# One group of norms ahead of the first table, and the routing check moved among the experts of layer 2

## The chip, the core and the metric

The kernel runs on one core of a Trainium2 chip. The metric is the device time in microseconds (us) from the start to the end of one execution. The engines of the core are named as the profile names them: PE (TensorE, matmuls; PEld are its weight loads), DVE (VectorE), ACT (ScalarE), POOL (GpSimd) and SP (SyncE, which here only issues DMAs; the profile calls its queue SPq). Each engine has its own instruction stream, and the streams are tied together by semaphores.

## What is computed

The reference is a network of four layers on a graph of 3125 nodes with 256 features and 50000 edges. Each layer adds a graph convolution and a mixer to `x`, and then a feed-forward block:

```python
xn = _layernorm(x)
x = x + gnn(xn, src, dst, ...) + mix(xn)
x = x + ffn(_layernorm(x))          # layers 0 to 2; layer 3's ffn routes by its own graph
```

Three pieces matter here. Layer 0's graph convolution multiplies the normed nodes with four relation matrices (256 x 256 each), and edges then fetch rows of the result. Layer 2's feed-forward block runs six experts on all nodes, each made of three 256 x 256 products with a relu after the first two, and adds the experts' outputs with routing weights that are zero for all but the best two. Layer 3's feed-forward block has a second edge list of 32768 edges (`edge_index` of `L3_ffn`), over which it runs a small graph attention.

## The kernel before, in words

Nodes are laid out in 25 tiles of 128, and most loops go over `GROUPS`: six groups of four tiles and a last one of a single tile. The whole of `x`, its layer norm `xn` and the transposed `xnT` stay in on-chip memory. All matmuls are fp32 and most are recorded under line 110, in the helper `mm`. The trace shows each of these as two records, so x8 in a row of it are four matmuls of the program.

**The start.** `build` (L2620) loads `x` and the four relation matrices (`relw`), loads the edge lists, and then runs `norm_x`, which for each group calls `norm_tiles` (L165 to L178): statistics and scaling on DVE, a square root on ACT, eight PE transposes, and two copies of the transposed tiles by ACT and DVE. After all seven groups come the tables: `fill` (L1001) makes for each tile two products of 512 columns (each two matmuls), has ACT copy them to `htab_s`, and SP writes 512 KB to `h_tab` in DRAM. Between the third and the fourth group stands `regular` (L2370), which checks that the edges are sorted and evenly spread: DVE builds one-hot rows (`ct_oh`, L610) that PE sums (L612), PE transposes the destinations (L2335), and they go through DRAM and back (L2337, L2339) so that each can be compared with its neighbour. Its verdict `ok` decides by `tc.If` between `fast` and `general`. With these inputs `fast` runs.

**Order.** The instructions are issued as written only on POOL (`manual_schedule`). On the other engines a planner of the compiler puts them in an order of its own, from the order in which the program emits them and the dependencies. What stands in an engine's stream then is fixed.

**Layer 2's experts and the routing of layer 3.** `l2_ffn` (L1673) computes the routing weights and then loops over six experts and, in each, over seven blocks of 512 nodes (the last has 128): four matmuls of 512 columns with `w1`, four with `w2`, and for each of four tiles two of 256 columns with `w3`. ACT applies the relus (L1710), and DVE adds to `x` (L1717). In the first expert two more PE instructions per tile add a bias. In the last expert `after2` norms each block and fills two more tables, `tab3` and `self3` (L901), from which layer 3 gathers.

Beside this the 256 columns of layer 3's second edge list are scattered into sorted order: `send4` yields one indirect DMA after the other (`by_dst`, L357, 128 rows of 8 bytes each, issued by POOL). The class `Pump` (L2691) counts the columns of the products that `mm` emits, and each time the count passes its limit it takes the next scatter from the generator and makes it wait for that product:

```python
    def after(self, product, n):
        self.seen += n
        if self.seen >= self.columns:
            self.seen -= self.columns
            i = next(self.gen, None)
            if i is not None:
                ...
                self.tc.add_manual_dep(i, product.name, info, reason="in time with the products")
```

The router's products count 6400 columns, each expert's 38400.

After the experts comes `route_check` (L2086), in a pool `chk4` of its own. SP loads the sorted list back (`rec`, L696), with a wait for all 256 scatters. DVE copies the destinations to `rc_d` (L2095); PE transposes them in four pieces (L2335), each copied by ACT or DVE to `od_dc` and written to DRAM (L2337); SP loads them shifted (`od_dh`, L2339); three DVE instructions compare neighbours (`od_jk`, L2342 to L2345); PE sums the bad ones (L2361); and DVE writes `ok4` (L2364), which is read only after layer 3's gathers, at the next `tc.If`.

**Layer 3's beginning.** `seg_near` (L434) gathers rows of `tab3` on POOL (L447) and sums them on PE with one-hot matrices (L430) that DVE makes (L416). Beside it `l3_mix` takes statistics of `xn` (`l3a_st`, L149), scales (`hb`, L1791 and L1794, on DVE), and has PE transpose the result (L165) and multiply it with `wx`.

Of the kernel before, what the change touches and what calls it, by code (L numbers as in the profile page):

```python
# [33 lines left out]
GROUPS = [(t, min(4, T - t)) for t in range(0, T, 4)]  # L34
# [55 lines left out]
def wtile(ap):  # L90

    return ap.rearrange("(k p) f -> p k f", p=P)


class Net:
    def __init__(self, tc, a, out):
        self.tc, self.nc, self.a, self.out = tc, tc.nc, a, out
        self.flip = 0
        self.apart = {}
        self.one_hots = 8  # L100
        self.pump = None
# [1375 lines left out]
    def l1_ffn(self, pool, after=None):  # L1477
# [66 lines left out]
        for b0, w in BLOCKS:  # L1544
            t0, n = b0 // P, w // P
            zb = pool.tile([P, 4, D], F32, name="z", bufs=2)
            z, full = zb[:, :n], [P, n, D]
            nc.vector.tensor_add(z, self.xn[:, t0:t0 + n], b2c[:, None, :].to_broadcast(full))
            for s in range(2):
                hT = pool.tile([P, 4, 512], F32, name="hT", bufs=2)  # L1550
                for f in range(4):
                    p = self.ps(w)
                    self.mm(p, [(W1[s][:, k, f * P:(f + 1) * P], self.xnT[:, k, b0:b0 + w]) for k in range(2)])
                    nc.scalar.activation(hT[:, f, :w], p, AF.Gelu, bias=B1[s][:, f:f + 1])  # L1554
                for i in range(n):
                    p = self.ps(D)
                    self.mm(p, [(hT[:, f, i * P:(i + 1) * P], W2[s][:, f, :]) for f in range(4)])
                    behind.append((z[:, i, :], p, wts[s]))
                    if len(behind) > 1:
                        add(*behind.pop(0))  # L1560
                    yield
            add(*behind.pop(0))
            self.ln_rows(pool, lambda i: z[:, i, :], lambda i: z[:, i, :], "l1z", n)
            nc.vector.tensor_mul(z, z, gam[:, None, :].to_broadcast(full))
            nc.vector.tensor_add(z, z, bet[:, None, :].to_broadcast(full))
            nc.vector.tensor_add(self.x[:, t0:t0 + n], self.x[:, t0:t0 + n], z)
            if after is not None:
                after(t0, n)
# [104 lines left out]
    def l2_ffn(self, pool, after=None):  # L1673
# [23 lines left out]
        for e in range(NE):  # L1697
# [4 lines left out]
            for b0, n in BLOCKS:  # L1702
                h = None
                for j, b in enumerate((b1, b2)):
                    o = pool.tile([P, 2, 512], F32, name=f"h{j}", bufs=2)
                    for f in range(2):
                        p = self.ps(n)
                        self.mm(p, [(w[j][:, k, f * P:(f + 1) * P],
                                     self.xnT[:, k, b0:b0 + n] if h is None else h[:, k, :n]) for k in range(2)])
                        nc.scalar.activation(o[:, f, :n], p, AF.Relu, bias=b[:, 2 * e + f:2 * e + f + 1])  # L1710
                        yield
                    h = o
                for i in range(n // P):
                    t = b0 // P + i
                    p = self.ps(D)
                    self.mm(p, [(h[:, k, i * P:(i + 1) * P], w[2][:, k, :]) for k in range(2)])
                    nc.vector.scalar_tensor_tensor(self.x[:, t, :], p, r[:, t, e:e + 1], self.x[:, t, :],  # L1717
                                                   op0=OP.mult, op1=OP.add)
                    if e == 0:
                        p = self.ps(P, parts=NE)  # L1720
                        nc.tensor.transpose(p, r[:, t, :], self.ident)
                        rT = pool.tile([NE, P], F32, name="rT", bufs=2)
                        nc.vector.tensor_copy(rT, p)
                        p = self.ps(D)
                        nc.tensor.matmul(p, rT, b3, start=True, stop=True)
                        nc.vector.tensor_add(self.x[:, t, :], self.x[:, t, :], p)
                    yield
                if e == NE - 1 and after is not None:
                    after(b0 // P, n // P)
# [665 lines left out]
    def fast(self):  # L2395

        nc, tc, a = self.nc, self.tc, self.a
        g = self.g
        with tc.tile_pool(name="keepf", bufs=1) as keep, tc.tile_pool(name="dramf", bufs=1, space=DRAM) as dram:
            self.dram = dram  # L2400
            tp = lambda name: tc.tile_pool(name=name, bufs=1)
# [6 lines left out]
            ok4 = keep.tile([P, 1], I32, name="ok4")  # L2408
# [50 lines left out]
            with Banks(self, **plain):  # L2459
                route = tp("route")  # L2460
                rec4, place4 = self.route_lists(route.__enter__())
                by_dst = dram.tile([P * C2, 2], F32, name="by_dst")
# [3 lines left out]
                send4 = self.send(by_dst, place4, rec4, C2)  # L2466
# [33 lines left out]
            with Banks(self, **plain):  # L2500
                with tp("set3") as sp, tp("ffn2") as p:
                    tab, fill3 = self.linear_table("tab3", sp, self.load(sp, "wl", wtile(a["L3_gnn_W_lT"])))
                    own, fill_own = self.linear_table("self3", sp, self.load(sp, "wr", wtile(a["L3_gnn_W_rT"])),
                                                      self.rowb(sp, "L3_gnn_b_l"))

                    def after2(t0, n):
                        self.norm_tiles(t0, n)
                        fill3(t0, n)
                        fill_own(t0, n)
                    self.pump = Pump(tc, send4, 760)  # L2510
                    for _ in self.l2_ffn(p, after2):
                        pass
                    self.pump = None
                    for _ in send4:
                        pass
                with tp("chk4") as p:
                    self.route_check(p, by_dst, ok4)
            route.__exit__(None, None, None)
            order.__exit__(None, None, None)

# [99 lines left out]
    def build(self):  # L2620
        nc, tc, a = self.nc, self.tc, self.a
        with tc.tile_pool(name="keep", bufs=1) as keep, tc.tile_pool(name="dramk", bufs=1, space=DRAM) as dramk:
            self.keep, self.dramk = keep, dramk
            self.constants(keep)
            self.x = keep.tile([P, T, D], F32, name="x")
            for t0, n in GROUPS:
                nc.sync.dma_start(self.x[:, t0:t0 + n, :],
                                  a["x"][t0 * P:(t0 + n) * P, :].rearrange("(t p) f -> p t f", p=P))
            self.g = {"n": C1, "tiles": T, "src": self.load(keep, "e1src", a["src"], dtype=I32)}
            self.xn = keep.tile([P, T, D], F32, name="xn")  # L2630
            self.xnT = keep.tile([P, 2, NP], F32, name="xnT")
            self.ln = (keep.tile([P, T, 6], F32, name="ln_st"), keep.tile([P, T, 2], F32, name="ln_mv"),
                       keep.tile([P, T], F32, name="ln_rs"))
            self.mixed = set()
            self.rdeg = keep.tile([P, T], F32, name="rdeg")
            self.deg = keep.tile([P, T], F32, name="deg")
            with Banks(self, mm=6), tc.tile_pool(name="reg", bufs=1) as p:
                fill = self.l0_table(p)
                self.destinations(p)
                self.norm_x()  # L2640
                for i, (t0, n) in enumerate(GROUPS):
                    if i == 3:
                        ok = self.regular(p, self.g)
                    fill(t0, n)
                ok = self.value(ok)
            with tc.If(ok > 0) as branch:
                with tc.manual_schedule(engines={mybir.EngineType.Pool}):
                    self.fast()
            with branch.Else():
                self.general()  # L2650
            o = self.out[:(T - 1) * P, :].rearrange("(t p) f -> p t f", p=P)
            nc.sync.dma_start(o, self.x[:, :T - 1, :])
            nc.sync.dma_start(self.out[(T - 1) * P:, :], self.x[:TAIL, T - 1, :])
# [37 lines left out]
class Pump:  # L2691


    def __init__(self, tc, gen, columns):
        self.tc, self.gen, self.columns, self.seen = tc, gen, columns, 0

    def after(self, product, n):
        self.seen += n
        if self.seen >= self.columns:
            self.seen -= self.columns  # L2700
            i = next(self.gen, None)
            if i is not None:
                info = mybir.DependencyInfo(mybir.DependencyClass.Sync, mybir.DependencyReason.DATA)
                self.tc.add_manual_dep(i, product.name, info, reason="in time with the products")

# [91 lines left out]
```

## Time and profile before

| what | us |
|---|---|
| three runs | 4594.84, 4579.54, 4588.5 (median 4588.5) |
| the profiled execution | 4591.9 |
| its span, first to last instruction | 4590.2 |
| PE busy in it | 3616.8 (79%) |
| POOL busy in it | 2612.1 (57%) |
| DVE busy in it | 2211.5 (48%) |

By stage, from the trace (us from the start of the span):

| stage | from | to | PE busy | DVE busy | POOL busy |
|---|---|---|---|---|---|
| norms, first table, edge check | 0 | 139.7 | 113.2 | 47.4 | 5.0 |
| layers 0 and 1, gathers of layer 2 | 139.7 | 2673.5 | 1866.0 | 1444.4 | 1705.2 |
| layer 2: router and first expert | 2673.5 | 2832.8 | 139.3 | 34.7 | 57.4 |
| layer 2: experts 1 to 4 | 2832.8 | 3103.4 | 269.4 | 47.1 | 194.4 |
| layer 2: last expert, with norms and tables | 3103.4 | 3255.2 | 131.1 | 55.0 | 0.0 |
| routing check, begin of layer 3's mixer | 3255.2 | 3302.5 | 18.7 | 43.8 | 21.3 |
| layer 3: gathers and mixer | 3302.5 | 3932.0 | 547.0 | 290.2 | 364.1 |
| layer 3: feed-forward block | 3932.0 | 4590.2 | 532.3 | 249.0 | 264.6 |

A row of the timeline gives the start, the length, the engine, the line and operation, out and in tiles, the count of merged instructions, and in square brackets the idle time before it with what ended it. A busy PE is not a PE at its peak, since the ends of its matmuls are modelled.

### The profile page before, as it was taken

How to read it: one execution, taken by the hardware profiler on the slowest of the kernel's cores; microseconds unless marked ns; L12 is line 12 of the kernel's file. 1: busy time of each engine (PE TensorE's matmuls, PEld its weight loads, DVE VectorE, ACT ScalarE, POOL GpSimd, SP SyncE). 2: the span in 40 equal slices, each digit the busy share in tenths (PEclk: the TensorE clock that was granted, in tenths of full speed). 3: DMA queues.
4: the chain of work that ended last, by engine and by line, in shares of the span. 5: the costliest groups of instructions: out<-in, count | busy, mean ns of one | idle time of the engine just before them, and what ended most of it. 6: DMA issues, size and time to landing. Idle time of an engine off the chain costs nothing. (4 is left out here: it accounts for less than half of the span.)

```text
span 4590.2 us, 47080 instructions
## 1 busy us (share of the span) xinstructions
PE 3616.8 (79%) x13977; PEld 2403.7 (52%) x13977; DVE 2211.5 (48%) x7451; ACT 749.8 (16%) x1455; POOL 2612.1 (57%) x2605
## 2 busy tenths in 40 slices
PE   7889876954877867677777679998699995389898
PEld 3457543633545545455455334555476773257665
DVE  4477431145777775883545342113665233515443
ACT  2010001211100112113111011222122220013222
POOL 0577776755777747565777524770376565226550
PEclk9889977976978878788998868999799998588888
DMA  3433343314433420123333300001233233200000
GB/s 123 160 96 101 103 122 99 110 49 127 133 101 104 109 63 21 31 50 97 103 110 107 111 21 8 15 8 37 84 111 109 82 98 114 59 4 10 8 8 29
DMA packets 231200, 348.62 MB, mean 76 GB/s; under 512 B 74128, under 2 KB 168135, under 8 KB 230936
## 3 DMA queue, kind: packets, MB, share of 16 engines
q0 software_dynamic: 108384, 219.50, 17.5%
q1 hardware_dynamic: 118136, 121.97, 8.6%
q10 hardware_dynamic: 4416, 4.01, 0.3%
q8 instruction: 118, 1.93, 0.2%
q14 instruction: 146, 1.20, 0.1%
HBM read 294.62 MB, written 50.61 MB: 75 GB/s over the span
## 5 line engine op out<-in xcount | busy, mean ns | idle before, releaser
L430 PE MATMUL seg<-G,E 128*128 128x256 f32 (+1 forms) x3210 | 917.6, 417 | 217.0 <-DMA G<-tab,e3src 85.2
L430 PEld LDWEIGHTS seg<-G,E 128*128 128x128 f32 x3210 | 601.7, 202 | 500.9 <-issue 134.3
L110 PE MATMUL mm<-xnT,w 128*128 128x512 f32 (+1 forms) x1232 | 540.5, 586 | 20.9 <-DVE x L2226 20.5
L447 POOL DMA_INDIRECT G<-h_tab,gi x391 | 386.0, 987 | 264.7 <-DMA selfw<-in_L_gnn_self_W 136.9
L416 DVE TENSOR_SCALAR E<-iota_row,e1dl 128x128 f32<-128x128 f32 (+1 forms) x1173 | 365.1, 321 | 354.1 <-PE seg L430 343.5
L357 POOL DMA_INDIRECT by_src<-rec,place x391 | 419.3, 1073 | 188.9 <-PE mm L110 121.0
L447 POOL DMA_INDIRECT G<-tab,e1src x391 | 383.9, 982 | 202.6 <-PE seg L430 131.0
L842 POOL DMA_INDIRECT ring<-l1rows,e1src x391 | 423.6, 1083 | 132.0 <-issue 54.2
L447 POOL DMA_INDIRECT G<-tab,e3src x391 | 387.6, 991 | 123.3 <-PE seg L430 65.5
L430 PE MATMUL seg<-ring,E 128*128 128x264 f32 (+1 forms) x1762 | 424.5, 381 | 31.2 <-DVE E L416 21.2
L110 PE MATMUL mm<-w,hT 128*128 128x256 f32 (+1 forms) x1712 | 398.2, 385 | 0.5 <-ACT hT L1554 0.5
L357 POOL DMA_INDIRECT by_dst<-rec,place x256 | 251.5, 982 | 240.1 <-PE mm L110 196.0
L842 POOL DMA_INDIRECT ring<-l3rows,e2src x256 | 248.2, 970 | 225.8 <-PE seg L430 155.8
L430 PEld LDWEIGHTS seg<-ring,E 128*128 128x128 f32 x1762 | 309.5, 213 | 117.1 <-DVE E L416 47.5
L110 PEld LDWEIGHTS mm<-xnT,w 128*128 128x128 f32 x1232 | 236.9, 205 | 248.6 <-issue 217.8
L110 PEld LDWEIGHTS mm<-w,hT 128*128 128x128 f32 (+1 forms) x1712 | 319.0, 190 | 59.1 <-issue 16.9
L165 PE MATMUL mm<-ident,xn 128*128 128x128 f32 x400 | 95.1, 393 | 226.5 <-DVE xn L178 223.3
L418 DVE TENSOR_SCALAR E<-iota_row,e3dl,rec 128x128 f32<-128x128 f32 (+1 forms) x391 | 144.1, 381 | 218.9 <-PE seg L430 217.2
L1717 DVE SCALAR_TENSOR_TENSOR x<-mm,l2t_r,x 128x256 f32<-128x256 f32 x150 | 70.8, 482 | 299.7 <-PE mm L110 299.7
L165 PEld LDWEIGHTS mm<-ident,xn 128*128 128x128 f32 x400 | 65.9, 191 | 256.1 <-DVE xn L178 175.2
L854 DVE TENSOR_TENSOR ring<-ring,ex 128x260 f32<-128x260 f32 (+1 forms) x647 | 192.2, 319 | 2.4 <-ACT ex L834 2.3
L1710 ACT ACTIVATE h<-mm,b 128x512 f32<-128x512 f32 (+1 forms) x168 | 107.2, 641 | 361.2 <-PE mm L110 360.9
(710 smaller groups left out, 4962.5 us busy)
## 6 DMA issues: line engine op xcount, KB each, us to landing
w<-in_L_ffn_w SPq DMA_DIRECT2D x16, 1024.0 KB
h_tab<-htab_s SPq DMA_DIRECT2D x25, 512.0 KB
r_b<-rowa SPq DMA_DIRECT2D x64, 128.0 KB
bn_h<-c_h SPq DMA_DIRECT2D x50, 128.0 KB
G<-h_tab,gi POOLq DMA_INDIRECT x391
by_src<-rec,place POOLq DMA_INDIRECT x391
ring<-l1rows,e1src POOLq DMA_INDIRECT x391
G<-tab,e3src POOLq DMA_INDIRECT x391
```

The costliest lines, as they stand in the source:

```text
L110: m = self.nc.tensor.matmul(out, l, r, start=(i == 0), stop=(i == last))
L165: self.nc.tensor.transpose(p[:, i * P:(i + 1) * P], src(t0 + i)[:, k * P:(k + 1) * P], self.ident)
L357: return self.nc.gpsimd.indirect_dma_start(out=table, out_offset=bass.IndirectOffsetOnAxis(ap=idx, axis=0), in_=src, in_offset=None, bound ...
L416: self.nc.vector.tensor_scalar(e[:, :w], self.iota2[:, :w], g["dl"][:, c:c + 1], None, op0=OP.is_equal)
L418: self.nc.vector.tensor_scalar(e[:, :w], self.iota2[:, :w], g["dl"][:, c:c + 1], weight[:, c:c + 1], op0=OP.is_equal, op1=OP.mult)
L430: self.nc.tensor.matmul(A[t], e, rows_c, start=first, stop=last)
L447: nc.gpsimd.indirect_dma_start(out=ring[i % len(ring)][:, :D], out_offset=None, in_=table, in_offset=bass.IndirectOffsetOnAxis(ap=gidx[:, ...
L842: nc.gpsimd.indirect_dma_start(out=ring[:, i % RING].rearrange("p h f -> p (h f)"), out_offset=None, in_=table, in_offset=bass.IndirectOff ...
L854: nc.vector.tensor_mul(r[:, :, :d + 1], r[:, :, :d + 1], ex[:, c, :, None].to_broadcast([P, 4, d + 1]))
L1710: nc.scalar.activation(o[:, f, :n], p, AF.Relu, bias=b[:, 2 * e + f:2 * e + f + 1])
L1717: nc.vector.scalar_tensor_tensor(self.x[:, t, :], p, r[:, t, e:e + 1], self.x[:, t, :], op0=OP.mult, op1=OP.add)
```

## The change

There are two independent edits.

At the start, `norm_x` is gone. Group by group, the norms of group i are emitted and then the table of group i - 1, and `regular` is emitted behind the norms of group 4 and the table of group 3. The last table follows the loop.

In layer 2, the limit of the pump is 640 columns in place of 760. `Pump` now tells when its generator has run out, with a flag `done`; the first product behind the last scatter's at which the count passes the limit sets it. The loop over `l2_ffn` looks at the flag at each step and emits `route_check` right there, once, in its pool `chk4`, which now lies inside the pools of the experts.

```diff
-                    self.pump = Pump(tc, send4, 760)
+                    self.pump = Pump(tc, send4, 640)
                     for _ in self.l2_ffn(p, after2):
-                        pass
-                    self.pump = None
-                    for _ in send4:
-                        pass
-                with tp("chk4") as p:
-                    self.route_check(p, by_dst, ok4)
+                        if self.pump is not None and self.pump.done:
+                            self.pump = None
+                            with tp("chk4") as cp:
+                                self.route_check(cp, by_dst, ok4)
+                    assert self.pump is None
...
                 fill = self.l0_table(p)
                 self.destinations(p)
-                self.norm_x()
                 for i, (t0, n) in enumerate(GROUPS):
-                    if i == 3:
+                    self.norm_tiles(t0, n)
+                    if i:
+                        fill(*GROUPS[i - 1])
+                    if i == 4:
                         ok = self.regular(p, self.g)
-                    fill(t0, n)
+                fill(*GROUPS[-1])
                 ok = self.value(ok)
...
     def __init__(self, tc, gen, columns):
-        self.tc, self.gen, self.columns, self.seen = tc, gen, columns, 0
+        self.tc, self.gen, self.columns, self.seen, self.done = tc, gen, columns, 0, False
...
-            i = next(self.gen, None)
-            if i is not None:
+            i = next(self.gen, self)
+            if i is self:
+                self.done = True
+            elif i is not None:
```

## The prediction

> **What bounds the kernel now.** I read the page's busy times first: PE is busy 79% of the span, and the chain of waits that ended last is almost all PE, so what counts is where PE stands idle or works on less. The two edits touch three stretches, so I then read these alone. First the start, in the view of windows (start and end, length, then busy time and count of PE, PEld, DVE, ACT and POOL, the granted clock, the share of DMA, GB/s):
>
> ```profile
> 0.00:31.00 31.00, 12.15 (x51) 9.72 (x52) 24.79 (x101) 6.80 (x15) 5.00 (x23) 1.00 0.45 153
> 31.00:72.90 41.90, 41.90 (x98) 18.39 (x98) 6.55 (x21) 13.70 (x25) 0.00 (x0) 1.00 0.35 138
> 72.90:91.10 18.20, 11.13 (x27) 2.66 (x26) 15.38 (x32) 1.02 (x3) 0.00 (x0) 0.61 0.18 54
> 91.10:139.70 48.60, 47.97 (x105) 20.80 (x105) 0.68 (x3) 15.21 (x26) 0.00 (x0) 0.94 0.32 130
> ```
>
> PE has 12 us of work in the first 31, while DVE norms; then 48 table matmuls fill it, the edge check holds it for 18.2 us, and 52 more fill it. The end of this stage is PE's.
>
> Second, the timeline of layer 2's experts, which shows the pace of both sides of the pump:
>
> ```profile
> 2832.83 3.70 PE L110 MATMUL mm<-xnT,w 128*128 128x512 f32 x8
> 2882.99 0.98 POOL L357 DMA_INDIRECT by_dst<-rec,place  x1 [0.30 <-PE mm L110]
> 2884.28 0.98 POOL L357 DMA_INDIRECT by_dst<-rec,place  x1 [0.30 <-issue]
> 2885.57 0.98 POOL L357 DMA_INDIRECT by_dst<-rec,place  x1 [0.31 <-PE mm L110]
> 2886.86 0.98 POOL L357 DMA_INDIRECT by_dst<-rec,place  x1 [0.30 <-PE mm L110]
> ...
> 2900.55 3.60 PE L110 MATMUL mm<-xnT,w 128*128 128x512 f32 x8
> ...
> 3035.78 3.60 PE L110 MATMUL mm<-xnT,w 128*128 128x512 f32 x8
> 3039.21 3.78 PE L110 MATMUL mm<-h,w 128*128 128x512 f32 x8
> 3042.83 3.80 PE L110 MATMUL mm<-w,h 128*128 128x256 f32 x16
> ```
>
> The PE rows are where expert 1 begins, expert 2, and expert 4 with its first block. An expert takes 67.6 us for 38400 columns, 1.761 ns a column, with no gaps. POOL's rows stand 1.287 us apart even where they wait for nothing: 0.98 busy and 0.30 between. The limit of 760 columns is 1.338 us of PE, so POOL has been just able to follow.
>
> Third, the timeline of the check and of what follows it:
>
> ```profile
> 3259.18 0.34 SPq L696 DMA_DIRECT2D rec<-by_dst  x1
> 3262.06 0.27 DVE L2095 COPY rc_d<-rec 128x256 f32<-128x256 f32 x1
> 3262.65 0.39 PE L2335 MATMUL mm<-ident,rc_d 128*64 128x128 f32 x1 [7.44 <-DVE l3a_mv L150]
> 3267.76 0.66 SPq L2339 DMA_DIRECT2D od_dh<-dlin  x1
> 3270.87 0.68 DVE L2342 SCALAR_TENSOR_TENSOR od_jk<-od_dh 64x512 f32<-64x512 f32 x1
> 3274.29 0.59 PE L2361 MATMUL mm<-rc_b,ones 128*128 128x5 f32 x2 [8.76 <-DVE od_jk L2345]
> 3276.11 0.72 POOL L935 MEMSET bn_n<- 32x1 f32 x1 [16.12 <-DVE ok L2364]
> 3277.24 0.99 POOL L447 DMA_INDIRECT G<-tab,e1src  x1 [0.16 <-issue]
> ```
>
> From the load of the sorted list to the end of PE's sum are 15.7 us, nearly all latency. PE's stream stands behind it, and POOL's gathers wait for its verdict.
>
> **What the Trainium skill says.** "Perfetto Trace Analysis", DMA Instruction — SWDGE (GPSIMD): the end of such a row is when the descriptors are written, not when data has moved, so a scatter's 0.98 us is not its landing. The trace agrees: the last scatter into `l3seed` starts at 4000.11, and SP's load that waits for it goes out at 4002.29, 2.2 us later. "DMA: Bandwidth & Descriptors", Anatomy of one DMA: about 2.0 us fixed for each DMA, most of it the receipt of the write. The load of `rec` (256 KB) is issued at 3259.18 and used at 3262.06, 2.9 us. "TensorE: Matmul & The Clock Gate", Architectural detail: PE's queue can pull weight loads ahead, no more. So a matmul that waits holds the rest; at 3262 to 3274 nothing passes it. The same page, What's actually happening: the clock is halved after about 3.4 us of idleness and comes back after as long a busy time. In the edge check the granted clock is 0.61, and behind it ACT's copies of `htab_s` start at 94.99, 97.91 and 99.67 where two matmuls at full clock take 1.72: PE, free at 91.1, lost 3.2 us.
>
> **The start.** The changed program's instruction order on PE, as built: 16 transposes, 16 table matmuls, three times 8 transposes and 16 matmuls, the check, 8 transposes, 16, 2, 20. The first matmul needs `relw`. The DMA view of the first 35 us shows about 370 GB/s until 16.6, with the 0.2 MB of `e1dst` last; by its bytes the first two of `relw`'s four loads are in by 13.9 and all by about 16. So two matmuls run before 16.1 and 98 from there, where 100 started at 30.9: 14.8 + 2 x 0.86 = 16.5 us. Against that, 34 transposes now stand between matmuls. Eight cost 1.41 (at 3140.31) to 1.97 us (at 16.02), so 34 cost 6.0 to 8.4; I take 7.0. Gain 9.5, with 6 (`relw` 2 us later, dear transposes) and 12 as ends. The check is the same work behind 64 matmuls instead of 48, 18.2 us again. Norms of groups 5 and 6 move on DVE behind the first two `ct_oh`, where it idled 35.6 us. ACT's load is 0.58 in 0.86 x 2 us, with copies of `xnT` between; it fits. On SP two writes to `dlin` now stand behind two of `h_tab`, and wait for DVE's memset at about 25 us; four buffers cover that.
>
> **Layer 2: the scatters.** 640 columns are 1.127 us of PE, less than POOL's 1.287. The router and expert 0 (44800 columns in 159 us) are slow enough, so POOL is on time at 2832.8, with scatter 70. The other 186 then follow at POOL's own pace: 186 x 1.287 = 239.4, so the last starts at 3072.2. PE passes the product that releases it, column 163840, at 3042.5, 29.7 us before. No product waits for POOL as such. Earlier in the queue, the router's `l2t` iota stands behind ten scatters instead of eight; that may cost 0.3 us, taken as nothing.
>
> **Layer 2: the check.** The generator is seen to be empty at column 164480, and there the program emits the check. The instruction order shows it whole: in expert 4, block 0, after two matmuls of 256 columns, PE has the four transposes and the sum of the check in one row, and then the products go on. So PE gets there at 3043.8. DVE holds `x`'s updates, ACT two copies, and SP has issued the last expert's weights; all stop with PE, and expert 4 waits for them. The chain: last scatter 3072.2; load of `rec` 2.2 later, 3074.4; from there 15.7 as before, less 1.5 since DVE has no statistics between its three `od_jk` (2.0 us instead of 3.4), 14.2: 3088.6. DVE first waits for two iotas behind the last scatter on POOL, until about 3074; its casts end before `rec` lands. PE stalls 3088.6 - 3043.8 = 44.8 us (40 to 49). Then the halved clock: 3.2 us (0 to 6). In sum +48.0.
>
> **Layer 3.** PE's 47.3 us at 3255.2 to 3302.5 were not all the check's. DVE needs its 25 statistics, then scales and adds group by group, 4.5 us each, and PE's transposes follow it. Without the check's work, DVE's remaining 16 statistics (0.39 us each) end at 3262.1, the root and four one-hots at 3263.3, the first scaled group at 3267.7, in place of 3275.59: 7.9 us. Some 1.0 us of one-hots also leave the chain of the groups. I take 8.5. POOL's gathers may start when the last table lands, 3259.4, so at 3260.5, 16.7 us earlier; that is the upper end, since DVE is last. The lower is 5. From 3302 on PE is 90% busy, so the gain holds.
>
> **Sum.** -9.5 + 48.0 - 8.5 = +30.0 us on the profiled execution's 4591.9: 4621.9. The median of the runs shown is 3.4 below that execution, so I predict 4618.5.
>
> **Rivals.** *POOL keeps pace* (this one is not slower). If back-to-back scatters took 1.127 us or less, the last would start at 3042.7, the check would end at 3059.1, and PE would lose 15.3 + 3.2 = 18.5: -9.5 + 18.5 - 8.5, 4589. It decides from that spacing on; 29.5 us hang on it. For it: one cannot see POOL's pace free of PE's for a long row. Against: no two in the timeline stand under 1.28 apart, those marked "issue" too. *The start gives nothing*: `relw` lands late, or transposes between matmuls cost waits: 4628. For it: no table matmul before 30.9 exists to show it. Against: the DMA's bytes. *Both gains are at their upper end* (12 and 16): 4588.5 - 12 + 48 - 16 = 4608.5. For it: POOL's wait for the verdict; against: DVE is late in layer 3. That the check doesn't run beside the experts at all is not a rival: it is the forecast.
>
> **How the numbers follow.** Forecast 0.75, pace 0.10, start nothing 0.08, both gains 0.07. This kernel's measurement tells 0.3% (13.8 us) from no change. Pace gives 0.07 within and 0.03 faster; of the rest, 0.06 falls within by a stall and clock at their low ends with both gains high, 0.01 faster. So faster 0.04, same 0.13, slower 0.83. The range: all low ends give 4588.5 + 40 - 12 - 16 = 4600.5, all high 4588.5 + 49 + 6 - 6 - 5 = 4632.5; with 6 us for the spread of runs and not all ends together, 4603 to 4634.
>
> **What would show it.** Right: the first table matmul at about 14 to 16 us and the branch near 130; scatters 1.287 apart from expert 1 on; one PE idle time of some 45 us in front of the check's transposes in expert 4, ended by DVE's `rc_d`; no check at the end of layer 2, gathers about 17 and first transposes about 8 us sooner after it. Wrong: scatters closer than 1.2 us, or products between the check's instructions on PE.

## The result and the profile after

| | median us | runs |
|---|---|---|
| before | 4584.2 | 4 (4579.5 to 4594.8) |
| after | 4621.5 | 4 (4611.6 to 4630.2) |

The ratio is 1.0077, with a 95% interval of 1.0048 to 1.0107: 22 to 49 us slower, in the middle 35 to 37. The profiled execution took 4611.55, its span is 4609.8; that is 19.6 more than the span of the profiled execution before.

**The start.** The view of windows of the kernel after, cut where PE's table matmuls begin, where the check of the edges begins and ends, and where the tables end (columns as in the prediction):

```profile
0.00:15.30 15.30, 4.03 (x16) 2.80 (x16) 10.84 (x48) 3.29 (x6) 5.00 (x23) 1.00 0.85 286
15.30:75.90 60.60, 60.56 (x153) 27.97 (x154) 19.67 (x73) 20.43 (x39) 0.00 (x0) 1.00 0.34 136
75.90:94.10 18.20, 10.16 (x28) 2.67 (x26) 15.18 (x32) 1.02 (x3) 0.00 (x0) 0.68 0.18 54
94.10:129.00 34.90, 34.90 (x83) 16.14 (x83) 1.66 (x5) 10.70 (x19) 0.00 (x0) 0.92 0.30 121
```

PE is full from 15.3 on; the check takes the same 18.2 us as before; the last product ends at 129.03 instead of 139.07. That is 10.0 us gained. The first tables in the timeline of PE, before and then after:

```profile
30.89 42.13 PE L110 MATMUL mm<-relw,xnT 128*128 128x512 f32 x96
```

```profile
15.34 16.86 PE L110 MATMUL mm<-relw,xnT 128*128 128x512 f32 x32 [1.91 <-DMA relw<-in_L_gnn_rel_W]
32.03 1.04 PE L165 MATMUL mm<-ident,xn 128*128 128x128 f32 x8
32.91 13.90 PE L110 MATMUL mm<-relw,xnT 128*128 128x512 f32 x32
```

The 1.00 that the view gives for the clock of the first two windows is no measurement at their beginning: the trace's record of the granted clock only starts at 21.16 us, and before that the same matmuls take longer (the two rows of 32).

**The check in layer 2.** The timeline of the kernel after around it (engines picked, in order of time):

```profile
3012.80 3.60 PE L110 MATMUL mm<-xnT,w 128*128 128x512 f32 x8
...
3019.85 0.59 PE L110 MATMUL mm<-w,h 128*128 128x256 f32 x2
3020.79 0.70 PE L110 MATMUL mm<-w,h 128*128 128x256 f32 x2 [0.35 <-ACT h L1710]
...
3048.91 0.98 POOL L357 DMA_INDIRECT by_dst<-rec,place  x1 [0.30 <-issue]
3050.20 0.98 POOL L357 DMA_INDIRECT by_dst<-rec,place  x1 [0.30 <-issue]
3052.45 0.34 SPq L696 DMA_DIRECT2D rec<-by_dst  x1
3055.10 0.29 DVE L2095 COPY rc_d<-rec 128x256 f32<-128x256 f32 x1 [1.50 <-DMA rec<-by_dst]
3055.45 0.42 PE L2335 MATMUL mm<-ident,rc_d 128*64 128x128 f32 x1 [33.96 <-DVE rc_d L2095]
...
3065.56 0.59 PE L2361 MATMUL mm<-rc_b,ones 128*128 128x5 f32 x2 [7.35 <-DVE od_jk L2345]
3066.00 4.44 PE L110 MATMUL mm<-w,h 128*128 128x256 f32 x12
3070.28 3.60 PE L110 MATMUL mm<-xnT,w 128*128 128x512 f32 x8
```

PE ends its last product at 3021.5 and stands 33.96 us in front of the first transpose, while POOL still issues scatters, 1.287 apart and each ready to go at once ("issue"). From the end of that product to the next (3066.0) are 44.5 us, against 44.8 forecast. The last scatter starts 28.7 us after PE has arrived: that is the lag, and the rest, 15.8 us, is the chain from there through the load and the check. Then the 12 records at 3066.00 take 4.28 until the next row, where 12 of the 16 in a row of 3.63 take 2.72: 1.6 us of slow clock.

**Layer 3's beginning,** in the timeline of the kernel after:

```profile
3277.49 0.59 PE L110 MATMUL mm<-wr,xnT 128*128 128x256 f32 x2
3282.90 0.99 POOL L447 DMA_INDIRECT G<-tab,e1src  x1 [0.45 <-issue]
3287.89 3.56 PE L430 MATMUL seg<-G,E 128*128 128x256 f32 x8 [9.80 <-DVE hb L1791]
3292.04 0.67 PE L430 MATMUL seg<-G,E 128*128 128x256 f32 x2 [0.60 <-DMA G<-tab,e1src]
3292.55 1.04 PE L165 MATMUL mm<-ident,hb 128*128 128x128 f32 x8
...
3317.09 3.48 PE L110 MATMUL mm<-xnT,wx 128*128 128x512 f32 x6 [0.29 <-issue]
```

The rows of the kernel before, for the same places:

```profile
3254.61 0.59 PE L110 MATMUL mm<-wr,xnT 128*128 128x256 f32 x2
3275.59 1.94 PE L165 MATMUL mm<-ident,hb 128*128 128x128 f32 x8 [0.71 <-DVE nb_s L2363]
3302.53 3.60 PE L110 MATMUL mm<-xnT,wx 128*128 128x512 f32 x8
```

From the last product of the tables (end 3278.1) to the first transposes of `hb` are 14.5 us instead of 20.4, to the matmuls with `wx` 39.0 instead of 47.3: 8.3 gained. The first gather goes out 4.8 us after that product, where it took 22.0.

**Where the 19.6 us of the two profiled executions lie.** Taken at the same instructions of both, the kernel after is ahead by 10.0 at the end of the tables; by 14.1 at the router of layer 2; by 23.0 at expert 1; then 22.9 behind at the end of layer 3's tables, 14.6 behind at the matmuls with `wx`, 19.6 behind at the end. So -10.0, +45.9 and -8.3 stand where the edits are. The other steps are -4.0, -8.9 and +5.0 in code that is the same in both. The largest of these, router and expert 0, is PE's clock, as the number behind the busy times of the five engines (the granted clock) shows, in the windows before:

```profile
2673.51:2832.83 159.32, 139.27 (x366) 68.92 (x366) 34.74 (x103) 24.70 (x41) 57.43 (x59) 0.79 0.06 14
```

and after:

```profile
2659.44:2809.84 150.40, 129.84 (x365) 62.73 (x365) 34.55 (x103) 24.60 (x41) 69.26 (x71) 0.86 0.06 15
```

The same matmuls took 139.3 us of PE at a clock of 0.79 and 129.8 at 0.86. The edits need not have done this: over all the traces of this case, from the router's first instruction (L1691) to the last update of `x` by expert 0, the stretch takes 145 to 165 us at clocks of 0.87 to 0.74, in no order of the limit, and a run with the limit of 640 alone takes as long as the kernel before (153.8 at 0.80 both). Without these three steps the edits make +27.5 in this pair, inside the interval of the runs.

### The profile page after: what moved, and what is told of

Same layout as the page of the kernel before. It is cut to its first block, busy times and chain, and to the rows that moved or that the text cites. A ratio compares the mean times of both kernels' runs of the same rounds, so it can differ in the third digit from the quotient of the medians.

```text
span 4609.8 us, 47036 instructions
## 1 busy us (share of the span) xinstructions
PE 3621.9 (79%) x13977; PEld 2403.7 (52%) x13977; DVE 2216.0 (48%) x7451; ACT 748.8 (16%) x1455; POOL 2612.4 (57%) x2605
## 5 line engine op out<-in xcount | busy, mean ns | idle before, releaser
L430 PEld LDWEIGHTS seg<-G,E 128*128 128x128 f32 x3210 | 606.8, 204 | 501.8 <-issue 148.4
L1717 DVE SCALAR_TENSOR_TENSOR x<-mm,l2t_r,x 128x256 f32<-128x256 f32 x150 | 70.8, 482 | 290.0 <-PE mm L110 290.0
```

What stands on the lines that cost most here:

```text
L430: self.nc.tensor.matmul(A[t], e, rows_c, start=first, stop=last)
```

## The experiments

They ran on four chips (0, 2, 9 and 15 in the record), on which the kernel before takes 5064 to 5117 us, a tenth more than in the result. So only ratios to the kernel before on the same chip count, and stretches inside one trace. These chips are called the second kind here, and the one of the result the first chip. The record has no number for the first chip, so a kind may be a condition of a chip and not the chip itself; and it has no trace of the kernel before from the second kind. "Expert time" below is the time from DVE's last update of `x` (L1717) in one expert to the last in the next.

### The two edits apart

The start's edit alone, with layer 2 as in the kernel before:

```diff
-                self.norm_x()
                 for i, (t0, n) in enumerate(GROUPS):
-                    if i == 3:
+                    self.norm_tiles(t0, n)
+                    if i:
+                        fill(*GROUPS[i - 1])
+                    if i == 4:
                         ok = self.regular(p, self.g)
-                    fill(t0, n)
+                fill(*GROUPS[-1])
```

> Only the edit of the start; layer 2 as before. The forecast's theory: PE's table products begin near 15 us instead of 31 and the branch comes about 10 us sooner, so about 10 us less in all (ratio near 0.998), and from the branch on the timeline is that of before moved by those 10 us. Rival (the start gives nothing, and what the changed kernel's timeline shows there is lost again before layer 2): first gathers of layer 1 and of layer 2 at the same time as before, total within 3 us.

Measured: 0.998 (0.9963 to 0.9997), 10 us of 5067 (2 to 19). The first gathers of layer 0 go out at 134.5 us; in the traces of the same chip with the start as before, at 147.1 and 148.4. The start's gain is real, and as far as the interval tells it is kept to the end.

The edit of layer 2 alone is the rest of the change's diff.

> Only the edit of layer 2; start as before. The forecast's theory: one idle time of PE of 34 us before the check's first transpose and 45 us from the last product before the check to the next one, 1.6 to 3 us of slow clock behind it, and 7 to 9 us back in layer 3: +37 to +40 us (ratio near 1.0085). Rival (the two edits hang together, the loss comes partly from the earlier start): the idle time is much under 34 us and the total under +25 us.

Measured: 1.0124 (1.0093 to 1.0156), some 63 us and so more than the 37 to 40 expected, and not in the expected place. PE stood only 5.2 us before the first transpose and 16 us from product to product. The lag was gone, since POOL was not behind: experts 1 to 3 had become slow themselves, 87.3, 89.7 and 89.3 us instead of 69.3, 67.6 and 67.6 on the first chip. Neither theory had this.

### The pace of the scatters alone

```diff
-                    self.pump = Pump(tc, send4, 760)
+                    self.pump = Pump(tc, send4, 640)
```

in the kernel before, with the check behind the experts.

> The kernel of before with the limit of 640 columns alone; the check stays behind the experts. The forecast's theory: POOL falls behind, but nobody waits for it before the experts end, so scatters stand 1.287 us apart from expert 1 on, the last starts some 25 us sooner than before, and the total is that of before within 3 us. Rival (the closer scatters themselves slow the experts, by their descriptors or the DMA they share): the experts take over 67.9 us each and the total is 5 us or more longer.

Measured: 1.0085 (1.0058 to 1.0112), and 1.0061 (1.0039 to 1.0082) in a second run, `pump640_again`. The forecast's theory fails on these chips; as the rival had it, the experts are slower, 88 to 89 us each. Its reason, descriptors or shared DMA, is not shown by this. The timeline of this kernel shows how (one block of expert 1):

```profile
3177.95 3.60 PE L110 MATMUL mm<-xnT,w 128*128 128x512 f32 x8
3179.63 0.98 POOL L357 DMA_INDIRECT by_dst<-rec,place  x1 [0.30 <-issue]
3182.61 1.26 ACT L1710 ACTIVATE h<-mm,b 128x512 f32<-128x512 f32 x2 [7.41 <-PE mm L110]
3182.75 0.98 POOL L357 DMA_INDIRECT by_dst<-rec,place  x1 [2.14 <-PE mm L110]
3183.35 3.70 PE L110 MATMUL mm<-h,w 128*128 128x512 f32 x8 [1.81 <-ACT h L1710]
```

By the profile's (modelled) ends, PE's first product of the block is done after half of the row of 3.60, at about 3179.8, and all four matmuls by 3181.5. ACT, idle for 7.41 us, starts its relu at 3182.61 only, POOL its next scatter at 3182.75. In the trace's records of semaphores, the updates that PE sends for the matmuls that ended from 3179.0 to 3181.5 all stand between 3182.49 and 3182.61. So the news that the matmuls are done comes up to 3.5 us after their modelled ends, to ACT, DVE and POOL alike; PE then waits for ACT. Whether the news alone is late, or already the end of the matmuls, the trace doesn't tell, since these ends are modelled; PE's matmuls start at their usual 0.43 us apart until 3180.95.

The block is no single case: of the 18 full blocks of experts 1 to 3, the relu starts more than 2.5 us after the first matmul in 12. In the two traces of the first chip it does so in none of 18 (1.98 to 2.08 us).

The same limit on the first chip costs nothing in the experts: in the trace of the changed kernel, experts 2 and 3 take 67.6 us each beside scatters 1.287 apart.

> The limit of 640 alone, check at the end, again. On a chip where the kernel before takes about 4585 us and an expert 67.6 us: the forecast's theory says same as before within 3 us, scatters 1.287 us apart with the last one about 30 us behind its product. If the slow experts (88 us) belong to the limit and not to the chip, they are seen here too, and the total is 30 us longer.

> The edit of layer 2 alone, again. On a chip with 67.6 us an expert: 34 us of idle time before the check's first transpose, 45 us from product to product, +37 to +40 us in all. On a chip where experts take 88 us beside the scatters: 16 us from product to product and the rest in the experts.

Both fell on a chip whose experts are slowed. Measured for the limit alone: 1.0061, as said above; for the edit of layer 2: 1.0111 (1.0068 to 1.0153).

### The changed kernel at other limits

`Pump(tc, send4, 760)` in the changed kernel, the check still where the scatters end:

> The changed kernel with the limit put back to 760 columns; the check is still emitted where the generator ends. The forecast's theory (the stall is POOL's lag plus a fixed chain of about 16 us): POOL has no lag at 760, so the check stands at the end of expert 4 and PE loses 15 to 16 us from product to product instead of 45, plus 2 us of slow clock; 29 us less than the changed kernel, about 4 us more than before less 3 for noise: -2 to +4 us against before. Rival (the stall comes from the check's place and its own waits, not from the pace of the scatters): PE again loses 40 us or more, total near that of the changed kernel.

Measured: 0.9994 (0.998 to 1.0009), 3 us less than before. The timeline of this kernel:

```profile
3442.75 0.70 PE L110 MATMUL mm<-w,h 128*128 128x256 f32 x2 [0.35 <-ACT h L1710]
3448.33 0.42 PE L2335 MATMUL mm<-ident,rc_d 128*64 128x128 f32 x1 [4.88 <-DVE rc_d L2095]
...
3458.50 0.59 PE L2361 MATMUL mm<-rc_b,ones 128*128 128x5 f32 x2 [7.40 <-DVE od_jk L2345]
3458.95 4.43 PE L110 MATMUL mm<-w,h 128*128 128x256 f32 x12
```

From the end of the last product (3443.45) to the next are 15.5 us: this is the chain without a lag, as the theory had it (15 to 16). On this kind of chip the lag was absent at 640 columns too (16 us in the edit of layer 2 alone), so it is the first chip's trace, and not the step from 640 to 760, that shows what the lag costs.

704 columns:

> The changed kernel with a limit of 704 columns, between 640 and 760. If PE runs its products without pauses (1.761 ns a column), POOL falls behind by 193 x 1.287 - 193 x 704 x 0.001761 = 9 us, and PE stands 9 - 1.2 + 15.8 = 24 us between the products around the check, half way between 45 and 15.7. If PE's products are slowed during the scatters, as in the runs before this one (73 us an expert and more), POOL has no lag at 704 either, and it is the chain alone, 16 us; then what is lost lies in the experts, between the expert's time at 760 (73 us) and at 640 (88 us). Rival (the stall belongs to the place of the check): 40 us or more.

Measured: 1.0036 (1.0018 to 1.0055). PE lost 14.1 us from product to product, the chain alone; experts 1 to 3 took 81.1, 78.8 and 83.0 us, between those at 640 and at 760. The theory's second branch holds, and the rival (40 us or more) falls.

### The check at another time, and in parts

Whole, but 28 steps of the loop over `l2_ffn` later (`wait` starts at 28):

```diff
-                        if self.pump is not None and self.pump.done:
-                            self.pump = None
-                            with tp("chk4") as cp:
-                                self.route_check(cp, by_dst, ok4)
+                        if self.pump is not None and self.pump.done:
+                            self.pump = None
+                        if self.pump is None:
+                            wait -= 1
+                            if wait == 0:
+                                with tp("chk4") as cp:
+                                    self.route_check(cp, by_dst, ok4)
```

> The changed kernel (640 columns), but the whole check is emitted 28 steps of the experts' loop later, about 37 us of PE. By the forecast's theory the list has landed by then, and only the chain inside the check is left, from the copy of the destinations to the sum: 10.5 us of PE in place of 45 (3 us of it work), about 32 us less than the changed kernel where PE is not slowed by the scatters, and 4 to 6 us less where it is. Rival (PE waits because POOL or DVE stands behind something else at the check): the idle time before the first transpose stays over 5 us.

Measured: 1.0042 (1.0025 to 1.0059). The timeline of this kernel:

```profile
3501.73 3.80 PE L110 MATMUL mm<-w,h 128*128 128x256 f32 x16
3505.36 0.27 PE L2335 MATMUL mm<-ident,rc_d 128*64 128x128 f32 x1
...
3514.99 0.59 PE L2361 MATMUL mm<-rc_b,ones 128*128 128x5 f32 x2 [7.38 <-DVE od_jk L2345]
3515.43 6.54 PE L110 MATMUL mm<-xnT,w 128*128 128x512 f32 x8
```

Nothing is idle before the first transpose now: the lag and the load of the list were what PE had waited for there. The 7.38 us inside, from the transposes through DRAM to the sum, stay: from the first transpose to the next product are 10.1 us, forecast 10.5, and the next row takes 6.54 instead of 3.60. The changed kernel as such ran on no chip of the second kind, so the 4 to 6 us between them were not measured directly.

In four parts, again 28 steps later, `route_check` made a generator with a `yield` behind the copies, behind the load of `od_dh` and behind the comparison, and one part taken every 8 steps:

```diff
+                        if self.pump is None:
+                            wait -= 1
+                            if wait <= 0 and wait % 8 == 0:
+                                next(check, None)
```

> As the late whole check, but emitted in four parts (load and copies; transposes and DRAM; comparison; sum) with 8 steps of the experts' loop between them, so that products stand between the parts on PE. Theory: no wait of PE above 1 us is left, 3 us of work and small gaps; where PE is not slowed by the scatters, the start's 10 us and layer 3's 7 to 8 us remain: about 4584 - 17 + 4 = 4571 on a chip where the kernel before takes 4584 (ratio 0.997); where the scatters slow the experts, these lose what the limit of 640 columns alone lost (ratio 1.002 to 1.006). Rival (the check costs PE its latency wherever it stands): 10 us or more idle around it.

Measured: 1.0037 (1.0019 to 1.0056), in the range for a chip whose experts are slowed. The timeline of this kernel shows the check with products between its parts and no idle time at all:

```profile
3487.59 0.27 PE L2383 MATMUL mm<-ident,rc_d 128*64 128x128 f32 x1
3487.70 1.02 PE L110 MATMUL mm<-xnT,w 128*128 128x512 f32 x2
3488.56 0.27 PE L2383 MATMUL mm<-ident,rc_d 128*64 128x128 f32 x1
...
3507.74 0.28 PE L2410 MATMUL mm<-rc_b,ones 128*128 128x5 f32 x2
3507.88 1.96 PE L110 MATMUL mm<-h,w 128*128 128x512 f32 x4
```

Expert 4, which holds the check, takes 70.1 us; with the limit of 640 and the check behind the experts it took 69.0 to 69.3. The gain over the whole check is read from these traces: as runs, 1.0037 and 1.0042 are not apart.

The same four parts with 760 columns and `wait = 9`, so that they fall into the last expert:

> The check in four parts, with the limit at 760 columns as before, so that the parts fall into the last expert. Theory: no lag, no chain on PE, and the scatters at the pace of before: the start's 10 us and layer 3's 5 to 8 us are gained, 3 us are paid; 12 us less than before, ratio 0.9975 (0.996 to 0.999) on either kind of chip. Rival (the last expert, with its norms and tables, has no room for the check on DVE): ratio 0.999 or more.

Measured: 0.996 (0.9941 to 0.9979), 20 us less than before (11 to 30, expected 12); the start's edit alone gave 10. The rival falls. The idle times at the check are 0.35 to 0.38 us between the transposes; the last expert takes 148.8 us, with the check behind it 146.8.

Without the edit of the start:

> The start as before; the limit at 760 columns; the check in four parts in the last expert. It leaves layer 3's gain alone: POOL's gathers about 16 us and the first scaled group about 8 us sooner after the last table, 3 us paid for the check in the last expert. Theory: 4 to 7 us less than before (ratio 0.9985 to 0.999). Rival (what layer 3's beginning gains is lost again further on, so that the better version lives from the start alone): ratio 1.000 or more.

Measured: 0.9999 (0.998 to 1.0018). This doesn't decide: the interval holds both. Within its trace, the first gather of layer 3 goes out 4.5 us after the last write of `self`, with the start's edit alone 21.2, and the last gather 655 us after it, there 670 (a trace of another chip); two us are paid in the last expert. So most of layer 3's gain is there in the trace, but the runs alone don't show it.

### Scatters further apart

The start's edit alone, with `Pump(tc, send4, 880)`:

> The start edit alone with a limit of 880 columns (check at the end as before): the scatters stand further apart than before, 43.6 in an expert instead of 50.5, and reach into the last expert. Here it is the slow experts that are asked about: an expert took 88 to 90 us at 640 columns, 79 to 83 at 704, 72 to 77 at 760, 67.6 with no scatter. If it is the density of the scatters that slows them, experts 1 to 4 take 68 to 70 us, and the total is 5 to 14 us less than with the start edit alone (ratio 0.995 to 0.997 to before). Rival (each scatter costs PE the same 0.1 us whatever its distance): 72 us an expert, and total as with the start edit alone (0.998). On a chip with 67.6 us an expert beside the scatters: no difference to the start edit alone.

Measured: 0.9932 (0.9912 to 0.9952), 34 us less than before; against the start's edit alone that is some 24 us, more than the 5 to 14 expected. Of these, 20 lie in experts 1 to 4 of the two traces. The numbers of experts 2 and 3, and in the last column of the 18 full blocks of experts 1 to 3:

| limit, columns | kernel, chip | scatters in an expert | experts 2 and 3, us | of it PE idle over 0.2 us at a time | relu over 2.5 us after the block's first matmul |
|---|---|---|---|---|---|
| 640 | check at the end, chip 2 | 60 | 89.3, 87.8 | 14.1, 12.3 | 12 of 18 |
| 704 | changed kernel, chip 9 | 54, 55 | 78.8, 83.0 | 8.5, 10.5 | 9 of 18 |
| 760 | start alone, chip 2 | 49, 51 | 72.1, 73.2 | 3.4, 4.4 | 7 of 18 |
| 880 | start alone, chip 0 | 44, 43 | 67.6, 67.8 | 0.2, 0.2 | 1 of 18 |

What the idle time leaves of the loss at 640 goes with the granted clock, 0.92 in expert 2 there and 1.00 at 880. The rows come from three chips. At 640 and 760 the other traces lie close to them (88.0 to 91.7 and 71.9 to 75.9 us in experts 2 and 3, on chips 2, 9 and 15); 880 ran on chip 0 alone. That chip 0 is of the second kind shows in its kernel before, 5064 us, and in this trace, where the first scatter of layer 2 starts at 2993 us, against 2985 to 3040 on the other three and 2663 to 2678 on the first chip.

The timeline of the kernel with 880:

```profile
3229.86 3.60 PE L110 MATMUL mm<-xnT,w 128*128 128x512 f32 x8
3229.88 0.98 POOL L357 DMA_INDIRECT by_dst<-rec,place  x1 [0.94 <-PE mm L110]
3231.84 0.69 ACT L1710 ACTIVATE h<-mm,b 128x512 f32<-128x512 f32 x1 [4.72 <-PE mm L110]
3233.30 3.78 PE L110 MATMUL mm<-h,w 128*128 128x512 f32 x8
```

ACT's relu starts 1.98 us after the block's first matmul; in the block shown at 640 columns it was 4.66. An eighth fewer scatters than at 760 take away the whole loss, so the rival (a fixed price for each) falls. The mean distance is not what differs most: in experts 1 to 3 the scatters start 1.47, 1.48 and 1.44 us apart at 640, 704 and 760, since a slowed PE asks for them more slowly, and 1.54 at 880. But at 640, 704 and 760 columns 77, 74 and 68 in a hundred follow the one before without rest (within 1.32 us), and at 880 47, with POOL resting between the others.

## Why the prediction was right

The forecast was 4618.5 (4603 to 4634), the measured median 4621.5. The steps, by their terms:

- **The start, -9.5: -10.0.** The place and the cause were right, but three parts of the sum were off and nearly cancelled, so its closeness is in part luck. The tables begin 15.55 us sooner, not 16.5: no two matmuls ran ahead of the rest. The 34 transposes took 4.6 us, not 7.0 (0.88 for eight, at 32.03, 46.64 and 61.25; 1.74 behind the check). And the table matmuls together took 1.0 us more than before, which the sum had at nothing: 15.55 - 4.6 - 1.0 = 10.0. PE's first 16 took 16.7 us from 15.34 on, where the next 16 took 13.7: their records stand 0.85 us apart until 21, then 0.43. That is the slow clock at the beginning, 3.0 us; in the kernel before it fell mostly on the transposes, where PE waited for DVE anyway. Two of the 3.0 come back: there the first rows of the tables were 0.8 slow, and behind the check part of the slow clock now falls on the transposes. The first table matmul at 15.34, ended by `relw`, lies in the 14 to 16 that were named.
- **The scatters.** 186 at 1.287 were to take 239.4 us from expert 1 on; the last started 240.4 after it. In the first chip's trace no product waits for POOL, as the step says.
- **The stall, 44.8: 44.5,** with one idle time of 33.96 before the transposes, ended by `rc_d`. From the load of `rec` to the end of the sum were 13.7, forecast 14.2. It splits as the working did, in 28.7 of lag (forecast 28.4, from 3043.8 to 3072.2) and 15.8 of chain (forecast 16.4).
- **The slow clock behind it, 3.2: 1.6,** inside its bounds of 0 to 6. The 3.2 was taken from the edge check, behind which full clock came back after 6.2 us (91.1 to 97.3 in the trace's record of the clock); behind this check it came after 3.3 (3066.0 to 3069.3). The record has the clock at 0.5 in both, so half of that is lost.
- **Layer 3, -8.5: -8.3.** The first transposes came 5.9 us sooner and not 7.9, since PE's stream has five matmuls on gathered rows (ten records) ahead of them, and one waits for its gather. The other 2.4 came between these transposes and the matmuls with `wx`, 24.5 us instead of 26.9, where the forecast had counted 1.0 at most: the sum was met, its parts were not. POOL's gathers came 17.2 us sooner, forecast 16.7.
- **Sum, +30.0: +27.5** at these places. The runs' medians say +37, with an interval from 22 to 49; the rest is in unchanged code, and no more than its clock was shown. That the median came within 3 us of 4618.5 is luck in part: the forecast started from a median of 4588.5 for the kernel before, which is 4584.2 with the fourth run.

The rival that POOL keeps pace is refuted by the row of scatters 1.287 apart with "issue", none of which, in experts 1 to 3, stands further from the one before. What neither the forecast nor a rival had is what the closer scatters do on the second kind of chip. There POOL gets no lag, because PE itself is slowed: PE waits for ACT, ACT for PE's late news. Layer 2's edit loses more there (1.011 to 1.012, 56 to 63 us, where the pair of traces of the first chip has 45.9 - 8.3 = 37.6). So the forecast's mechanism is shown for the kind of chip whose trace it was made from, and not for the other. There, less the start's 10, these runs give an estimate of 46 to 53 us for the whole change, but the changed kernel did not run.

Open is why PE's updates are late on the second kind of chip and not on the first, and whether that is the chip or something that ran beside it. Four limits show that on these chips it goes with scatters that leave POOL no rest; on the first chip scatters without any rest cost nothing. The traces of the second kind also lack records of PE's updates: in experts 1 to 3, 247 stand for 310 instructions with an update at 640 columns and 260 for 307 at 880, and on the first chip 309 for 309 and 310 for 310. So something differs there even where no expert is slowed; whether the recording itself has a part in the lateness was not tested. Version 880 with the check in parts was not tried, nor were 880 and the four parts on a chip of the first kind; there only the 10 us of the start and layer 3's gain are to be expected (an estimate from the result's pair of traces), since no expert is slowed.

## What to carry to other kernels

A step that is moved "beside" other work is beside it only if it is cut where it waits: a check with a trip through DRAM, put in one piece into PE's stream, cost its whole latency here (15.5 us, or 10.1 where its data had landed long before), and in four pieces with products between them about 1 to 2 us. Before pacing one engine by another's progress, compare the pace asked for with the follower's own back-to-back time (here 1.127 against 1.287 us), over the whole row: the lag grows with each instruction and is paid at the first wait for the last of them. And leave the follower some rest: on chips of the second kind, long rows of indirect DMAs without rest went with some 88 us an expert, where 67.6 were enough with rests, though PE and ACT have nothing to do with these DMAs.

## What was not expected of the hardware

On chips of the second kind, PE's semaphore updates reached ACT, DVE and POOL up to 3.5 us after the modelled ends of its matmuls while POOL issued indirect DMAs back to back, and nearly all on time when every second one or so had a rest before it (640 and 880 columns: 12 and 1 of 18 relus late, 88 to 89 and 67.6 us an expert). On the first chip the same row at 1.287 us apart left the experts at 67.6.

How long PE is slow after a wait varied by a factor of two. The Trainium skill, "TensorE: Matmul & The Clock Gate", What's actually happening, has full clock come back after at least one busy window of some 3.4 us. The trace's record of the clock, whose stretches are multiples of 3.4 us, has it 3.3 us after the first product behind layer 2's check, but 6.2 behind the edge check (kernel before), 5.8 behind the late whole check, and 5.8 after the first table matmul of the changed kernel: one or two of these steps. So the single busy time that the forecast took from the page is the least and not the rule. The four slow stretches cost 1.6, 3.2, 2.9 and 3.0 us on top of the wait.
